# A two-layer graph-attention kernel on one core: layer 1's sums placed next to the head products, PSUM places given out anew, and the turn of h moved within the step

## The chip, the cores and the metric

The kernel runs on one core of one Trainium2 chip. The metric is the device time of the program in microseconds (us), as a median of several executions. One further execution was recorded by the hardware profiler; its own time and span stand beside the median below. The engines are named as in the profile: PE (matrix products and transposes; PEld is its loading of weights), DVE (vector engine), ACT (scalar engine), POOL (GpSimd) and SP (which issues DMAs).

## The reference

The input is x, 16 graphs of 1024 nodes with 256 features each, and adj, a 1024 x 1024 integer matrix of 0 and 1 for each graph. Two layers follow each other, each with a layer norm and a ReLU ahead of it and a residual around it.

Layer 0 is masked attention with 8 heads of 32 features:

```python
h = jnp.maximum(_layernorm(x), 0.0)
Q, K, V = proj(Wq, bq), proj(Wk, bk), proj(Wv, bv)      # 8 heads of 32
scores = einsum('bhnd,bhmd->bhnm', Q, K) * SCALE
scores = where(adj == 0, -inf, scores)
out = einsum('bhnm,bhmd->bhnd', softmax(scores), V)
x = x + out @ Wo.T + bo
```

Layer 1 has scores that are made of the nodes themselves, one kind of score for each value of adj (with adj of 0 and 1 only one kind occurs, and the kernel holds a slower way for the others that is not taken):

```python
h = jnp.maximum(_layernorm(x), 0.0)
e = leaky_relu(einsum('bid,bjd->bij', h * a_0[:, 0], h), 0.2)
x = x + softmax(where(adj == 1, e, -9e15)) @ h
```

## The kernel before

A *tile* is 128 rows (nodes) of one graph; there are 8 tiles in a graph and 128 in all. The kernel is one software pipeline over tiles, written out by hand (`tc.manual_schedule()`): the instructions of each engine are executed in just the order in which the program emits them. The outer loop runs over tile steps s (lines 839 to 980), the inner one over the 8 heads h of the tile that is now attended, which I call head steps. In each head step several objects at different stages do a piece of their work:

- `now` (class `Attend`) is the tile s whose heads are scored. `scores(h)` (L461) puts 128 x 1024 scores on one of two PSUM sides, `softmax_max(h)` (L473, DVE) takes them from there with the mask, and `softmax_exp` (L490, ACT) follows one head step later. Heads 4 and 6 use one side, the others the other side, so the scores of a head wait until L473 of the last head on the same side is done.
- Two head steps after its scores, a head's probabilities are turned. Heads 0, 1, 4 and 5 are turned by DVE in blocks (L381) and put in place by DMAs on SP (L386); heads 2, 3, 6 and 7 by PE (L590) with copies on ACT (L591). In the last tile of a graph (tile 7) PE turns heads 4 and 5 too, and in tile 0 heads 0 and 1; their exps then change the order of elements.
- `combine(0)` (L526) makes the products of heads 0 to 3 with the values in head step 7; `was.combine(1)` makes those of heads 4 to 7 in head step 3 of the next tile step, after `recT` (L520), the reciprocals of the sums. Both use the array in 32 columns at a time (128*32 in the profile). `combined` (L536) multiplies, `output` (L541) makes y in head step 4, `residual` (L547) and `norms` follow on DVE in head step 5.
- `piece` (class `Piece`) is the tile 9 steps ahead, whose Q, K and V are made. `normed` (L223, ACT, head step 4) makes h, `turn` (L237, PE, head step 5) transposes it, `turned` (L249 and L250, ACT) copies it out twice as hT and hTm, `project(0, ...)` (L267, head step 6) makes K, `raised(0)` (L309, ACT, head step 7) takes K out of PSUM. As `piece_was` it goes on in the next tile step: Q by `project(1, ...)` in head step 1, taken out by `raised(1)` (L309) in head step 4, and V by `values` (L344) in head step 2, taken out by `biased` (L355).
- `edge` and `edge_was` (class `Edges`) are layer 1's tiles 9 and 10 steps behind. `edge` has its scores made (L627 and L633), its maximum taken (L656), bent (L665), its copies kept for the mirrored half (L647) and its exp (L680). `edge_was` has its probabilities turned in head step 0, and its sums are made by `gather(0)` and `gather(1)` (L698, 64 matmul instructions together in the profile, also 32 columns at a time). `store` (L705, L707 on DVE, L708 on SP) divides, adds the residual and sends the result out.

The mask of the next tile is made by `flag` (L453, ACT) and `mask` (L441, POOL) in head step 3. Gathers exist from s = 10 on; the piece ends with s = 118. After the loop a tail does layer 1 for the last graph's tiles.

PSUM is given out by hand: the two score sides, two rotating buffers for transposes, and two banks of two places each for all that is smaller. A wait between engines holds for a whole bank:

```python
banks = [ps_acc.tile([P, 2, D], F32, tag=f"acc{i}", ...) for i in range(2)]
sums_place, brief, early, late = (banks[i // 2][:, i % 2, :] for i in range(4))
```

Before the change, `sums_place` takes the head products and the gathers' sums, `brief` the turned h of layer 1 and the turned reciprocals, `early` Q, and `late` V, y, the turned h of the piece, and K.

Of the kernel before, what the change touches and what calls it, by code (L numbers as in the profile page):

```python
# [17 lines left out]
P = 128  # L18
# [12 lines left out]
def by_blocks(t):  # L31
    return BY_BLOCKS.get(t, MIXED)
# [15 lines left out]
def gnn_kernel(  # L48
# [46 lines left out]
    sums_place, brief, early, late = (banks[i // 2][:, i % 2, :] for i in range(4))  # L95
# [92 lines left out]
    class Piece:  # L188
# [66 lines left out]
        def project(self, which, oc):  # L255
            wT, bias = ((weights["wkT"], bk_t), (weights["wqT"], bq_t))[which]
            b, w = self.b, self.n * P
            if b not in kds:
                kds[b] = dram.tile([NC, P, 2, N], F32, tag="kd", name=f"kd_{b}")
            if b not in qds and which == 1:  # L260
                qds[b] = dram.tile([NT, NC, P, 2, 2, P], F32, tag="qd", name=f"qd_{b}")
            if self.n > 1:
                ps = ps_tr.tile([P, w], F32, tag="tr", name="proj")
            else:
                ps = (late, early)[which][:, oc * P : (oc + 1) * P]
            for fc in range(NC):
                nc.tensor.matmul(  # L267
                    ps,
                    lhsT=wT[:, fc, oc * P : (oc + 1) * P],
                    rhs=(self.hT, self.hTm)[which][:, fc, :],  # L270
                    start=(fc == 0),
                    stop=(fc == NC - 1),
                )

            self.projected.append((which, oc, ps, bias))
# [139 lines left out]
    class Attend:  # L415
# [120 lines left out]
            nc.vector.tensor_tensor(self.oT, by_chunk(sums_place), self.recT, ALU.mult)  # L536

        def output(self):
            self.y = late
            for g in range(NC):  # L540
                nc.tensor.matmul(  # L541
                    self.y, lhsT=self.oT[:, g, :], rhs=weights["woT"][:, g, :], start=(g == 0), stop=(g == NC - 1)
                )
# [50 lines left out]
    class Edges:  # L594


        def __init__(self, b, t, last=False):
            self.b, self.t, self.last = b, t, last
            self.rows = slice(t * P, (t + 1) * P)
            self.side = sides[t % 2 if last else 1]  # L600
            self.tags = {"sel": ("p", 4), "pT1": ("pT", 7)} if last else {}
            if last and t % 2:
                self.tags |= {"ha": ("hT", 1), "x1b": ("x1", 1), "h0": ("xb", 1)}
            self.sums = late if last and t % 2 else sums_place

        def buffer(self, tag, shape):
            tag, bufs = self.tags.get(tag, (tag, 1))
# [168 lines left out]
    def attend_of(s):  # L776
        return Attend(*divmod(s, NT)) if 0 <= s < B * NT else None
# [9 lines left out]
    with tc.manual_schedule():  # L787
        first = [Piece(0, 0, 4), Piece(0, 4, 4)]
        piece_was, piece_next = Piece(1, 0), piece_of(0)
        now, nxt = attend_of(0), attend_of(1)  # L790
# [39 lines left out]
        piece, edge, edge_was = piece_next, None, None  # L830
# [8 lines left out]
        for s in range(B * NT + 1):  # L839
            b, t = divmod(s, NT)  # L840

            def load_keys(h, end):
                if t == NT - 1 and b + 1 < B and 2 * h + end in KEY_STEPS:
                    load_key(b + 1, KEY_STEPS.index(2 * h + end))
                if t == 0 and 0 < b < B and 2 * (HEADS + h) + end in KEY_STEPS:
                    load_key(b, KEY_STEPS.index(2 * (HEADS + h) + end))

            nxt2, edge_nxt, piece_nxt = attend_of(s + 2), edges_of(s + 1), piece_of(s + 1)
            for h in range(HEADS):
                ending, eh = (now, h - 1) if h >= 1 else (was, HEADS - 1)  # L850
                turning, th = (now, h - 2) if h >= 2 else (was, HEADS + h - 2)

                load_keys(h, 0)


                if now:
                    now.scores(h)
                if h == 0 and piece_was:
                    piece_was.halve(0)
                if s == 0 and h == 1:  # L860
                    first[1].values()
                if h == 3 and edge:
                    edge.softmax_max()
                if h == 5:
                    if was:
                        was.residual()
                    norms(was, piece_nxt)
                if h == 6 and edge_was:
                    edge_was.gather(1)
                if now:  # L870
                    now.softmax_max(h)
                if h == 6 and edge_was:
                    edge_was.store()


                if h == 1 and edge:
                    edge.keep(0)
                if h == 2 and gone:
                    gone.turned_normed()
                if ending:  # L880
                    ending.softmax_exp(eh)

                if h == 3 and was:
                    was.turned_reciprocals()
                if h == 3 and edge:
                    edge.bend()
                    edge.keep(1)


                if h == 3:  # L890
                    if was:
                        was.combine(1)
                    if piece_was:
                        piece_was.biased()
                    if was:
                        was.combined()
                if turning and th in by_blocks(turning.t):
                    turning.turn_blocks(th)
                    turning.place_blocks(th)
                elif turning:  # L900
                    turning.turn(th, 0)
                    turning.turn(th, 1)


                if h == 0:
                    if edge:
                        edge.score(0)
                    if gone:
                        gone.normed()
                    if edge_was:  # L910
                        edge_was.turn_blocks()
                        edge_was.place_blocks()
                if h == 1:
                    if gone:
                        gone.turn_normed()
                    if piece_was:
                        piece_was.project(1, 0)
                        piece_was.project(1, 1)
                    if was:
                        was.reciprocals()  # L920
                    if piece_nxt:
                        piece_nxt.load()
                if h == 2:
                    if edge:
                        edge.score(1)
                    if piece_was:
                        piece_was.values()
                    if was:
                        was.turn_reciprocals()
                        was.add_bias()  # L930
                if h == 3:
                    if nxt:
                        nxt.load_queries()
                    if edge:
                        edge.leak()
                    if edge_was:
                        edge_was.load_nodes()
                    if nxt:
                        nxt.flag()
                        nxt.mask()  # L940
                if h == 4:
                    if was:
                        was.output()
                    if piece_was:
                        piece_was.raised(1)
                        piece_was.halve(1)
                    if piece:
                        piece.normed()
                    if piece_was:
                        piece_was.write_queries()  # L950
                    if edge_nxt:
                        edge_nxt.prepare()
                    if nxt2:
                        nxt2.load()
                if h == 5:
                    if edge_was:
                        edge_was.gather(0)
                    if piece:
                        piece.turn()
                    if piece:  # L960
                        piece.turned()
                if h == 6:
                    if edge:
                        edge.softmax_exp()
                    if was:
                        was.keep()
                    if now:
                        now.load_nodes()
                    if piece:
                        piece.project(0, 0)  # L970
                        piece.project(0, 1)
                if h == 7:
                    if now:
                        now.combine(0)
                    if piece:
                        piece.raised(0)
                load_keys(h, 1)
            gone, was, now, nxt = was, now, nxt, nxt2
            edge_was, edge = edge, edge_nxt
            piece_was, piece = piece, piece_nxt  # L980
# [84 lines left out]
```

## Time and profile before

| | |
|---|---|
| median of 3 runs | 3068.4 us (3067.28 to 3073.23) |
| the profiled execution | 3076.4 us |
| its span in the trace | 3074.5 us, 96254 instructions |
| mean granted clock of TensorE | 0.996 |
| L461, scores, x2048 | 760.6 us busy |
| L590, transposes of probabilities, x4608 | 604.5 us busy |
| L526, head products, x16384 | 533.4 us busy |
| L698, gathers, x8192 | 496.9 us busy |
| L473, maximum on DVE, x1024 | 1236.2 us busy |
| L490, exp on ACT, x1024 | 1249.4 us busy |

The table is read as follows. The span is the time from the first to the last instruction of the profiled execution. Busy time is the time in which at least one instruction of the group ran. PE's matmuls overlap, and their ends are modelled, so the distance between two starts says more of PE than a duration does. In the answers of the trace a line gives a start in us from the begin of the span, a duration, the engine, the line of the program, the operation, what it writes and reads, and how many instructions are merged in it. "[0.67 <-PE s L461]" says that the engine had been idle for 0.67 us and which result ended that.

### The profile page before, as it was taken

The page shows a single profiled execution, that of the slowest core. Times are in us where ns is not written, and L with a number is a line of the kernel's source. Part 1 is how long each engine was busy: PE and PEld are TensorE (multiplying, and loading weights), DVE is VectorE, ACT ScalarE, POOL GpSimd, SP SyncE. Part 2 cuts the span into 40 slices and gives each one's busy share as a digit, 9 for nine tenths or more (in the row PEclk, how much of TensorE's full clock was granted, in tenths as well). Part 3 has the DMA queues.
Part 4 walks back from the last instruction along what each step waited for, and adds up shares of the span by engine and source line. Part 5 has one row for each costly group of instructions (what it writes and reads, how often), then busy time and mean ns, then how long its engine had stood idle before and what let it go on. Part 6 is the DMA issues. An engine that isn't in the chain of part 4 may idle for free. (4 is left out here: it accounts for less than half of the span.)

```text
span 3074.5 us, 96254 instructions
## 1 busy us (share of the span) xinstructions
PE 2965.6 (96%) x36722; PEld 2230.1 (73%) x36722; DVE 2515.6 (82%) x4453; ACT 2654.5 (86%) x5159; POOL 2177.6 (71%) x2999
## 2 busy tenths in 40 slices
PE   7889999999999999999999999999999999999998
PEld 5667777777777777777777777777777777776664
DVE  5878888888888888888888788888888888888885
ACT  5888888899898998889889888988989888898882
POOL 3657777777777777777777777777777777776542
PEclk9999999999999999999999999999999999999999
DMA  7766777877777786777777777787777777777653
GB/s 245 219 219 205 237 235 222 255 216 243 231 225 243 230 257 209 232 247 220 246 230 228 235 232 243 221 255 221 220 247 228 251 211 235 237 227 236 191 168 100
DMA packets 597828, 695.68 MB, mean 226 GB/s; under 512 B 63280, under 2 KB 528560, under 8 KB 597360
## 3 DMA queue, kind: packets, MB, share of 16 engines
q1 hardware_dynamic: 528288, 477.29, 51.9%
q0 software_dynamic: 66960, 210.04, 21.0%
q8 instruction: 295, 4.83, 0.7%
q10 hardware_dynamic: 2112, 2.10, 0.2%
q14 instruction: 173, 1.42, 0.1%
HBM read 252.98 MB, written 134.22 MB: 126 GB/s over the span
## 5 line engine op out<-in xcount | busy, mean ns | idle before, releaser
L473 DVE CUSTOM_DVE_ANT_0 p<-s,neg 128x1024 f32<-128x1024 f32 x1024 | 1236.2, 1208 | 220.7 <-PE s L461 185.1
L490 ACT ACTIVATE p<-p,nmx 128x1024 f32<-128x1024 f32 x1024 | 1249.4, 1224 | 132.5 <-DVE nmx L473 123.9
L461 PE MATMUL s<-k,qt 128*128 128x512 f32 x2048 | 760.6, 453 | 15.5 <-DVE nmx L473 4.3
L591 ACT COPY pT<-trp 128x512 f32<-128x512 f32 x1024 | 549.4, 590 | 95.3 <-PE trp L590 94.9
L590 PE MATMUL trp<-ident,p 128*128 128x128 f32 x4608 | 604.5, 274 | 4.7 <-ACT pT L591 1.5
L590 PEld LDWEIGHTS trp<-ident,p 128*128 128x128 f32 x4608 | 531.0, 140 | 104.0 <-ACT pT L591 10.8
L381 DVE STREAM_TRANSPOSE blocks<-p 128x1024 f32<-128x1024 f32 x456 | 564.5, 1238 | 12.3 <-ACT p L680 10.6
L526 PE MATMUL acc<-pT,v 128*32 128x128 f32 x16384 | 533.4, 275 | 41.8 <-ACT recT L520 30.0
L526 PEld LDWEIGHTS acc<-pT,v 128*32 128x32 f32 x16384 | 453.5, 110 | 153.0 <-ACT recT L520 85.0
L698 PE MATMUL acc<-h,pT 128*32 128x256 f32 x8192 | 496.9, 382 | 2.8 <-DVE h L707 1.7
L441 POOL TENSOR_SCALAR neg<-adj 128x1024 bf16<-128x1024 int32 x128 | 467.9, 3655 | 42.9 <-ACT neg L453 33.7
L461 PEld LDWEIGHTS s<-k,qt 128*128 128x128 f32 x2048 | 322.9, 191 | 106.3 <-issue 43.0
L698 PEld LDWEIGHTS acc<-h,pT 128*32 128x32 f32 x8192 | 241.8, 109 | 207.8 <-issue 65.6
L676 POOL TENSOR_TENSOR sel<-sel,less 128x1024 f32<-128x1024 f32 x120 | 286.8, 2390 | 68.9 <-ACT less L665 47.6
L633 PE MATMUL s<-h1T,ha 128*128 128x512 f32 (+2 forms) x744 | 272.8, 490 | 2.7 <-ACT h1T L569 1.6
L674 POOL TENSOR_SCALAR less<-top 128x1 f32<-128x1 f32 x120 | 31.9, 266 | 274.0 <-DVE top L656 273.9
L324 POOL DMA_DIRECT2D qd<-halves x240 | 177.5, 780 | 58.7 <-POOL halves L314 31.8
L490 ACT ACTIVATION_READ_ACCUMULATOR p<-p,nmx 128x1 f32 x1024 | 206.8, 202 | 0.0
L510 POOL COPY wide<-rec 128x256 f32<-128x256 f32 x128 | 53.8, 420 | 204.2 <-DVE rec L508 204.2
L330 POOL DMA_DIRECT2D kd<-halves x240 | 172.2, 766 | 35.5 <-POOL halves L314 35.4
L314 POOL TENSOR_TENSOR halves<-full,halves 128x256 fp32r<-128x256 f32 x240 | 176.8, 737 | 20.6
L633 PEld LDWEIGHTS s<-h1T,ha 128*128 128x128 f32 x744 | 126.7, 190 | 70.7 <-issue 45.0
(117 smaller groups left out, 4328.4 us busy)
## 6 DMA issues: line engine op xcount, KB each, us to landing
pT<-blocks SPq DMA_DIRECT2D x2304, 128.0 KB, 3.5
qt<-qd SPq DMA_DIRECT2D x128, 512.0 KB, 4.5
k<-kd SPq DMA_DIRECT2D x128, 512.0 KB, 7.3
adj<-in_adj POOLq DMA_DIRECT2D x127, 512.0 KB, 5.0
qd<-halves POOLq DMA_DIRECT2D x240, 256.0 KB, 2.7
kd<-halves POOLq DMA_DIRECT2D x240, 128.0 KB, 4.1
xb<-in_x POOLq DMA_DIRECT2D x128, 128.0 KB, 4.2
x1d<-x SPq DMA_DIRECT2D x128, 128.0 KB, 4.0
```

Source lines behind the costliest of these rows:

```text
L324: nc.gpsimd.dma_start(out=qds[self.b][self.first, oc].rearrange("p u w n -> p u (w n)"), in_=halves.unsqueeze(1).to_broadcast([P, 2, 2 * P]),)
L381: nc.vector.transpose(blocks.rearrange("p b j q -> p j b q"), p)
L441: nc.gpsimd.tensor_scalar(self.neg, self.adj, 0.0, MASKED, ALU.is_equal, ALU.mult)
L461: nc.tensor.matmul(self.ps[:, cols], lhsT=self.qt[:, h, :], rhs=keysets[self.b][h][:, cols], start=True, stop=True,)
L473: nc.vector.tensor_tensor_reduce(out=p, in0=sides[h in self.second], in1=self.neg, scale=-SCALE, scalar=FLOOR, op0=ALU.add, op1=ALU.min, a ...
L490: nc.scalar.activation(to, of, AF.Exp, bias=nmx, scale=-1.0, accum_out=self.sums[:, h : h + 1])
L526: nc.tensor.matmul(sums_place[r * HD : (r + 1) * HD, g * P : (g + 1) * P], lhsT=vs[self.b][:, j, place_of(h) : place_of(h) + HD], rhs=self ...
L590: nc.tensor.transpose(tr[:, j, :], p[:, jj * P : (jj + 1) * P], ident)
L591: copy(pT[:, half * 4 : half * 4 + 4, :], tr)
L633: nc.tensor.matmul(self.side[:, cols], lhsT=self.ha[:, c, :], rhs=h1T[:, c, cols], start=(c == 0), stop=(c == NC - 1),)
L676: nc.gpsimd.tensor_tensor(self.sel, self.sel, self.less, ALU.subtract)
L698: nc.tensor.matmul(self.sums[a * HD : (a + 1) * HD, :], lhsT=self.pT[:, j, a], rhs=h1s[self.b][:, j, :], start=(j == 0), stop=(j == NT - 1),)
```

## The change

The change is in the order of emission and in the PSUM places; what is computed stays the same, and no instruction is added or dropped.

- Both gathers and the store move to head step 7. Before, `gather(0)` stood in head step 5 behind head 3's transposes, `gather(1)` in head step 6 behind the scores, and the store in head step 6. Now they stand together, directly ahead of `combine(0)`; K is made in head step 7 too, ahead of the gathers, and taken out (`raised(0)`) after the store.
- The places: the gathers' sums go to `early` (in the second bank), y and the piece's K to `brief` (in the first).
- `turn` and `turned` of the next h move ahead of head 3's transposes in head step 5, so L237 directly follows the scores of head 5 on PE, and L249 and L250 go ahead of head 3's copies on ACT.
- `softmax_max` moves ahead of residual and norms in head step 5.

On PE the order from head step 5 on was scores 5, L590, L698, L237, scores 6, L698, L267, scores 7, L526. It is now scores 5, L237, L590, scores 6, scores 7, L267, L698, L698, L526. In tile 7 the transposes of heads 4 and 5 stand directly behind scores 6 and 7.

```diff
@@ project
-                ps = (late, early)[which][:, oc * P : (oc + 1) * P]
+                ps = (brief, early)[which][:, oc * P : (oc + 1) * P]
@@ output
-            self.y = late
+            self.y = brief
@@ Edges
-            self.sums = late if last and t % 2 else sums_place
+            self.sums = (late if t % 2 else sums_place) if last else early
@@ the loop over heads
+                if now:
+                    now.softmax_max(h)
                 if h == 5:
                     if was:
                         was.residual()
                     norms(was, piece_nxt)
-                if h == 6 and edge_was:
-                    edge_was.gather(1)
-                if now:
-                    now.softmax_max(h)
-                if h == 6 and edge_was:
-                    edge_was.store()
...
+                if h == 5 and piece:
+                    piece.turn()
+                    piece.turned()
                 if turning and th in by_blocks(turning.t):
...
-                if h == 5:
-                    if edge_was:
-                        edge_was.gather(0)
-                    if piece:
-                        piece.turn()
-                    if piece:
-                        piece.turned()
                 if h == 6:
...
                     if now:
                         now.load_nodes()
+                if h == 7:
                     if piece:
                         piece.project(0, 0)
                         piece.project(0, 1)
-                if h == 7:
+                    if edge_was:
+                        edge_was.gather(0)
+                        edge_was.gather(1)
+                        edge_was.store()
+                    if piece:
+                        piece.raised(0)
                     if now:
                         now.combine(0)
-                    if piece:
-                        piece.raised(0)
```

## The prediction

> **What bounds the kernel now.** I read the busy shares first, then PE's order of time in one tile step (one pass of the loop over s), then the same step on ACT and DVE, then the waits.
>
> ```profile
> PE 2965.6 (96%) x36722; PEld 2230.1 (73%) x36722; DVE 2515.6 (82%) x4453; ACT 2654.5 (86%) x5159; POOL 2177.6 (71%) x2999
> ```
>
> PE has the least air, and in the timeline one of its groups follows the other. The step from 1455.26 us, head steps 5 to 7 and then the next step's head 0 (columns: start, duration, engine, line):
>
> ```profile
> 1455.26 0.81 PE L461 MATMUL s<-k,qt 128*128 128x512 f32 x2
> 1455.91 1.03 PE L590 MATMUL trp<-ident,p 128*128 128x128 f32 x8
> 1456.88 1.93 PE L698 MATMUL acc<-h,pT 128*32 128x256 f32 x32
> 1458.74 0.44 PE L237 MATMUL acc<-ident,h 128*128 128x128 f32 x2
> 1458.94 0.71 PE L461 MATMUL s<-k,qt 128*128 128x512 f32 x2
> 1459.58 1.93 PE L698 MATMUL acc<-h,pT 128*32 128x256 f32 x32
> 1461.44 1.16 PE L267 MATMUL acc<-hT,wkT 128*128 128x128 f32 x8
> 1462.36 0.71 PE L461 MATMUL s<-k,qt 128*128 128x512 f32 x2
> 1463.00 1.95 PE L526 MATMUL acc<-pT,v 128*32 128x128 f32 x64
> 1464.89 0.73 PE L461 MATMUL s<-k,qt 128*128 128x512 f32 x2
> ```
>
> From start to start (that is what PE pays) no group waits here. The narrow groups (128*32) come three times, each between wide ones (128*128). Ordinary steps (tiles 2 to 6 of a batch) repeat every 22.1 to 22.7 us, so a microsecond on this path is a microsecond of the step. On ACT, in the same step:
>
> ```profile
> 1455.90 0.65 ACT L309 ACTIVATE full<-acc,bq_t 128x128 f32<-128x128 f32 x2
> 1456.41 0.62 ACT L223 ACTIVATE h<-xin,shift,r 128x256 f32<-128x256 f32 x1
> 1456.90 1.16 ACT L490 ACTIVATE p<-p,nmx 128x1024 f32<-128x1024 f32 x1
> ```
>
> L223 makes the h that L237 turns. It ends at 1457.03, and L237 ran at 1458.74: 1.7 us of cover, given by head 3's transposes (L590) and the first gather (L698). The change takes both away.
>
> **Saved on PE: passages between narrow and wide.** Starts to starts, L590 takes 0.97 ahead of L698, but 0.87 ahead of a wide group (1465.46 to 1466.33); a score pair takes 0.64 ahead of a narrow group, 0.55 ahead of a wide one (1446.25 to 1447.07 and on to 1447.61 shows 0.82 for a projection and 0.54 for the pair). A gather of 32 takes 1.86. In the tail both gathers already run as one:
>
> ```profile
> 3019.12 3.66 PE L698 MATMUL acc<-h,pT 128*32 128x256 f32 x64 [1.74 <-DVE h L707]
> 3022.71 0.55 PE L627 MATMUL s<-ident,mirror 128*128 128x128 f32 x3
> ```
>
> 3.59 to the next wide group, against 2 x 1.86 = 3.72; followed by L526, narrow too, it also saves the passage out, 0.11 (within a gather four matmuls start every 0.216, the last four are followed by a wide start after 0.33): 3.48. New order from L237 to the next step's head 0: L237 0.22, L590 0.79 (0.08 less ahead of scores, as two transposes of L516 take 0.14 there), scores 6 0.63 (ahead of scores 7; no such neighbours in the trace, bounds 0.46 and 0.65, two starts 0.316 apart is what a pair shows inside), scores 7 0.55, L267 0.98, gathers 3.48, L526 1.87: 8.52. Before, L590 to head 0 is 1464.89 - 1455.91 = 8.98. **Saved 0.45 a step** (0.40 to 0.55). 109 tile steps (s = 10 to 118) have both gather and turn: **-49 us**.
>
> **Added: PE waits for h.** In the new order L237 follows scores 5, so it could start at 1455.91. L223 ends at 1457.03, and PE starts 0.05 after an ACT result (recT to L526, all 128 times): 1457.08. PE stands still for 1.17, and everything behind L237 with it: head 3's transposes, scores 6 and 7, gathers, products. Over all 120 turns the end of L223 lies 0.91 to 1.32 behind the start of the group after scores 5, mean 1.09. One part goes: L309 read `early` and waited for L541 writing `late` in the same bank; y is now in the other bank. Waits name it, "ACT full L309 <- PE acc L541", 8.5 us in all, 0.06 a step. **1.09 - 0.06 + 0.05 = 1.08; x 109 = +118 us.** Does ACT come earlier when PE is slower? The chain into L223 starts at PE's own scores 2:
>
> ```profile
> 1470.26 1.23 DVE L473 CUSTOM_DVE_ANT_0 p<-s,neg 128x1024 f32<-128x1024 f32 x1 [0.67 <-PE s L461]
> ```
>
> ```profile
> 1473.81 1.06 ACT L665 ACTIVATE less<-sel 128x1024 f32<-128x1024 f32 x1 [0.67 <-DVE top L656]
> ```
>
> From there L473, head 0's turn and L656 on DVE, then L665, mirror, mask flag, exp 3, two copies, L309, L223 on ACT run without a gap (in tile 0 with one of 1.0 for PE): 9.4 to 9.9 us from scores 2 to h. PE is waited for at its head, so the chain moves with PE and the wait repeats in each step.
>
> **Added: the batch's last tile.** In tile 7 heads 4 and 5 are turned by PE, and their exps, which change the order, take twice as long:
>
> ```profile
> 1501.70 2.26 ACT L490 ACTIVATE p<-p,nmx 128x1024 f32<-128x1024 f32 x1
> ...
> 1505.28 2.26 ACT L490 ACTIVATE p<-p,nmx 128x1024 f32<-128x1024 f32 x1
> ```
>
> ```profile
> 1506.43 1.09 PE L590 MATMUL trp<-ident,p 128*128 128x128 f32 x8
> ...
> 1508.72 1.03 PE L590 MATMUL trp<-ident,p 128*128 128x128 f32 x8
> ```
>
> Both L590 now find exp ready, because the gathers go ahead of them. Laid out anew: L309 has 0.29 less wait, so h at 1501.51, L237 1501.56, head 3 1501.78, scores 6 1502.57, turn of head 4 at 1503.17; exp 4 runs from 1501.41 to 1503.67, so 1503.72: 0.55 lost. Scores 7, then the turn of head 5 at 1505.06; exp 5 starts after exp 4 (2.11), L249, L250 (0.53) and two copies (0.94) at 1504.99 and ends 1507.25: 1507.30, 2.24 lost. **2.8 x 13 tiles = +36 us.**
>
> **Without gathers (s = 0 to 9).** Today L267 waits 1.64 there for hTm, which now comes ahead of head 3's copies; but L526 directly follows L267 and must wait for L309: both are in the first bank. From 118.05: h 119.33, L237 119.38, L267 to 122.35, exps 5 and 6 and L309 to 124.75, L526 124.80, next head 0 at 126.69 against 127.31: **-6 us** in all. Where gathers stand between them, L309 ends 0.13 before the gathers (1463.61 and 1463.74 by the rows above): no wait. The last nine steps have no turn: -4, and two tiles 7 with exp waits, +5: **+1**.
>
> The rows behind that bank wait are L309's 27 waits for L541, which write and read different columns. The Trainium skill, PSUM — Partial Sum Buffer, section "PSUM bank collisions raise a hardware error", says why: PSUM is to be guarded by bank and quadrant, not by address. That speaks against K in `brief` beside the products in `sums_place`; by address alone the first ten steps would be 2.25 faster each.
>
> **The rest at nothing.** L473 of head 5 goes ahead of residual and norms (1.55 on DVE): it ends near 1457.3, scores 7 need its side at about 1458.4; behind the 1.55 it would cost 0.4. L707 and L705 now stand right ahead of head 0's L473 on DVE: gathers end near 1463.8, L707 done by 1464.6, the scores that L473 needs land near 1466.3. On SP the store (L708) moves behind L552 and eight L386 loads and ahead of the sel blocks' four, whose data come over 2 us later; POOL gets head step 7's L309 earlier against head 0 (1.9 instead of 1.1).
>
> **Clock.** Long gaps lower it: with the 1.64 wait at 122 us the mean is 0.92, later 1.00.
>
> ```profile
> 119.00:140.00 21.00, 17.80 (x210) 14.62 (x209) 16.60 (x29) 17.39 (x37) 13.08 (x18) 0.92 0.67 208
> ```
>
> 8% of 21 us is 1.7 us. The same steps from 98 us show 1.00, so not every such wait does it. Tile 7's 2.24 may: 0 to 25 us for 15; I take **+10**, under a half.
>
> The Trainium skill, TensorE: Matmul & The Clock Gate, section "Why this matters for your kernels", asks only that gaps stay under about 3 us; by it this term is 0 and the sum 100. The row above contradicts that, so I keep the 10.
>
> **Sum:** -49 + 118 + 36 - 6 + 1 + 10 = **+110 us** on the profiled 3076.4, 3186; the runs' median 3068.4 is 8.0 lower: **3178 us**.
>
> **Rivals.**
> - *More waits* (0.14): L309 comes 0.4 later than laid out (margin 0.13); L526 waits 0.3 x 109 = 33 and the clock takes 25: 3226. For it: ACT is the fullest engine after PE. Against: DVE leaves it nothing to wait for in this stretch.
> - *h earlier* (0.14): ACT gains until only L541 holds L223 (1500.59 + 0.10 + 0.60 + 0.05 against 1500.90: 0.44 wait); 0.64 x 109 = 70 less: 3108. Against: ACT shows no gap between L665 and L309 in most steps.
> - *Faster* (0.08): h is there when scores 5 end. It decides once L237's wait is under 0.45, the saving. With no waits at all: 3068.4 - 49 - 6 = 3013. Against: 0.91 is the least seen.
> - *It doesn't do what it says* (0.04): waits inside the narrow run cancel the 0.45 and h hides: 3068.
>
> **Numbers.** Forecast 3178 with 0.60. Range 3095 to 3235: it takes in the unknowns (scores 6, clock, L309: 3140 to 3230) and the first two rivals, 0.88. Under 0.2%, 6 us, a measurement can't tell from no change: faster 0.08, same 0.04, slower 0.88.
>
> **What would show it.** Ordinary steps near 23.1 instead of 22.4; L237 and its weights idle some 1.1 us "<-ACT h L223"; L590 idle in tiles 7 behind ACT p; L698 x64 then L526 in one run of about 5.3. Wrong if L237 starts within 0.3 of scores 5, or if L526 waits for L309 in ordinary steps.

## The result, and the profile after

The changed kernel takes 3184.72 us (median of 4 runs, 3179.14 to 3185.3), the one before 3070.16 us in the runs beside it: a ratio of 1.0369, 95% interval 1.0351 to 1.0387. The prediction, 3178 us, lies 7 us below. The profiled execution has a span of 3183.5 us against 3074.5, at the same mean granted clock of 0.996.

The busy shares of the changed kernel, from its page:

```profile
PE 2938.4 (92%) x36722; PEld 2276.2 (71%) x36722; DVE 2511.9 (79%) x4453; ACT 2625.8 (82%) x5159; POOL 2177.5 (68%) x2999
```

Every engine has a smaller share of the span than before, and only PEld is busy for longer (2276.2 us against 2230.1), so the time went into waits. The timeline of PE in an ordinary step of the changed kernel, the same stretch as the one shown of before (start, duration, engine, line; in brackets the idle time ahead of the group and what ended it):

```profile
1515.08 0.82 PE L461 MATMUL s<-k,qt 128*128 128x512 f32 x2
1516.90 0.44 PE L237 MATMUL acc<-ident,h 128*128 128x128 f32 x2 [1.00 <-ACT h L223]
1517.17 1.04 PE L590 MATMUL trp<-ident,p 128*128 128x128 f32 x8
1517.97 1.18 PE L461 MATMUL s<-k,qt 128*128 128x512 f32 x4
1518.98 1.05 PE L267 MATMUL acc<-hT,wkT 128*128 128x128 f32 x8
1519.97 3.66 PE L698 MATMUL acc<-h,pT 128*32 128x256 f32 x64
1523.45 2.16 PE L526 MATMUL acc<-pT,v 128*32 128x128 f32 x64
1525.54 0.73 PE L461 MATMUL s<-k,qt 128*128 128x512 f32 x2
```

The first row starts at 1515.08, the second at 1516.90: 1.82 us for a group that takes 0.65. L237 waits for L223's h, as forecast. The gathers and the head products now run as one stretch of narrow matmuls, and from L698 to L526 it is the 3.48 of the forecast. L526 takes 2.09 to the next scores, though, where 1.87 was laid out. Why is seen in the waits (who waited, for what; us in total, times, longest):

```profile
PEld acc L237 <- ACT h L223: 162.1, 119, 1.9
...
PEld acc L526 <- ACT full L309: 53.6, 106, 3.6
```

```profile
PE acc L237 <- ACT h L223: 110.4, 119, 1.4
```

```profile
1522.74 0.66 ACT L309 ACTIVATE full<-acc,bk_t 128x128 f32<-128x128 f32 x2
```

The first line is the forecast wait, in 119 of the 120 turns. The second was forecast for the first ten steps alone: L526's weights wait for L309, K's taking out, in 106 steps. In the step above L309 ends at 1523.40 by its line, and L526 starts at 1523.45, 3.48 after the gathers. That is no wait to speak of, but the run of L526 takes 0.2 longer to the next scores.

In tile 7 PE waits twice more, in the two places that the forecast names:

```profile
1566.19 1.14 PE L590 MATMUL trp<-ident,p 128*128 128x128 f32 x8 [1.25 <-ACT pT L591]
...
1568.72 1.09 PE L590 MATMUL trp<-ident,p 128*128 128x128 f32 x8 [0.91 <-ACT p L490]
```

The second of these waits is for head 5's slow exp. The first is for head 3's copy, which stands behind head 4's slow exp on ACT and holds the buffer that the transposes of head 4 need.

The steps, from one tile's scores 5 to the next tile's, medians of 13 or 14 graphs:

| tile | 0 | 1 | 2 | 3 | 4 | 5 | 6 | 7 |
|---|---|---|---|---|---|---|---|---|
| before | 23.78 | 23.05 | 22.73 | 22.45 | 22.47 | 22.17 | 22.28 | 26.09 |
| changed | 23.76 | 23.55 | 23.66 | 23.40 | 23.40 | 22.98 | 23.14 | 29.56 |

### The profile page after: what moved, and what is told of

Its sections match the earlier page's. It is cut to its first block, busy times and chain, and to the rows that moved or that the text cites. A ratio compares the mean times of both kernels' runs of the same rounds, so it can differ in the third digit from the quotient of the medians.

```text
span 3183.5 us, 95926 instructions
## 1 busy us (share of the span) xinstructions
PE 2938.4 (92%) x36722; PEld 2276.2 (71%) x36722; DVE 2511.9 (79%) x4453; ACT 2625.8 (82%) x5159; POOL 2177.5 (68%) x2999
## 5 line engine op out<-in xcount | busy, mean ns | idle before, releaser
L591 ACT COPY pT<-trp 128x512 f32<-128x512 f32 x1024 | 553.4, 597 | 337.8 <-PE trp L590 337.6
L461 PE MATMUL s<-k,qt 128*128 128x512 f32 x2048 | 732.8, 447 | 14.6 <-DVE nmx L473 5.1
L590 PE MATMUL trp<-ident,p 128*128 128x128 f32 x4608 | 606.5, 274 | 37.4 <-ACT pT L591 20.9
L590 PEld LDWEIGHTS trp<-ident,p 128*128 128x128 f32 x4608 | 526.6, 140 | 126.2 <-ACT pT L591 37.1
L526 PE MATMUL acc<-pT,v 128*32 128x128 f32 x16384 | 547.6, 276 | 53.5 <-ACT recT L520 30.3
L526 PEld LDWEIGHTS acc<-pT,v 128*32 128x32 f32 x16384 | 470.8, 110 | 153.5 <-ACT recT L520 85.2
L698 PE MATMUL acc<-h,pT 128*32 128x256 f32 x8192 | 473.1, 381 | 1.6 <-DMA pT<-blocks 1.5
L461 PEld LDWEIGHTS s<-k,qt 128*128 128x128 f32 x2048 | 329.9, 190 | 110.0 <-issue 41.5
L698 PEld LDWEIGHTS acc<-h,pT 128*32 128x32 f32 x8192 | 255.3, 110 | 179.2 <-DMA pT<-blocks 6.8
L490 ACT ACTIVATION_READ_ACCUMULATOR p<-p,nmx 128x1 f32 x1024 | 221.3, 216 | 0.0
```

The costliest lines, as they stand in the source:

```text
L461: nc.tensor.matmul(self.ps[:, cols], lhsT=self.qt[:, h, :], rhs=keysets[self.b][h][:, cols], start=True, stop=True,)
L490: nc.scalar.activation(to, of, AF.Exp, bias=nmx, scale=-1.0, accum_out=self.sums[:, h : h + 1])
L526: nc.tensor.matmul(sums_place[r * HD : (r + 1) * HD, g * P : (g + 1) * P], lhsT=vs[self.b][:, j, place_of(h) : place_of(h) + HD], rhs=self ...
L590: nc.tensor.transpose(tr[:, j, :], p[:, jj * P : (jj + 1) * P], ident)
L591: copy(pT[:, half * 4 : half * 4 + 4, :], tr)
L698: nc.tensor.matmul(self.sums[a * HD : (a + 1) * HD, :], lhsT=self.pT[:, j, a], rhs=h1s[self.b][:, j, :], start=(j == 0), stop=(j == NT - 1),)
```

## The experiments

My theory at first was the forecast's: L237's wait for h costs the step its length. The rivals were that L237 waits for something else too, and, after the first experiment, that the step is set by another chain. The ratios are against the kernel before, which ran beside each of them (medians 3072 to 3080 us).

**1. The price of a passage, in the kernel before.** One passage from narrow to wide matmuls and back is added, by cutting the first gather in two.

```diff
-                        edge_was.gather(0)
+                        edge_was.gather(0, 0)
                     if piece:
                         piece.turn()
+                    if edge_was:
+                        edge_was.gather(0, 1)
```

> The kernel before with the turn of h (L237) between the two halves of the first gather instead of behind it: the same instructions, one narrow run more in each of 109 steps. Theory (each passage into and out of a narrow run costs PE 0.2 to 0.35 us): +22 to +38 us, 3100 us. Rival (a passage costs nothing by itself): 3066 to 3076.

Measured: 3100.11 us, ratio 1.0092 (1.0075 to 1.0109): +28 us in 109 steps, 0.26 a step; single steps grow by 0.31 in the median. The saving that the forecast counts on is real.

**2. The turn of h behind head 3's transposes again.** Everything else stays as changed, and ACT's order too.

```diff
-                    piece.turn()
-                    piece.turned()
+                    between = piece
...
+                        turning.turn_around(th, between)
...
+            for half in range(2):
...
+            piece.turn()
+            piece.turned()
+            for half, tr in enumerate(trs):
+                copy(pT[:, half * 4 : half * 4 + 4, :], tr)
```

> The changed kernel with one thing undone: on PE the turn of h (L237) stands behind head 3's eight transposes again; on ACT its two copies stay ahead of head 3's. Theory (PE stands still for h): 0.87 us of transposes cover the wait, which falls from 1.08 to some 0.2 in 96 ordinary steps, -83 us; nothing in tiles 7, where the turn of head 4 waits for its exp at the same time as before; -6 in the first ten steps: 3096 us (3080 to 3115). Rival (the 6.5 us from scores 7 to the next scores 0, in which PE makes no scores, starve DVE and ACT): that stretch is unchanged, so 3175 to 3190.

Measured: 3199.43 us, ratio 1.0413 (1.0392 to 1.0434), 15 slower than the changed kernel. Here my first theory fell. PE in an ordinary step (a new function stands in this program, and the lines behind it are higher by 15: L506, in it, is head 3's transposing, L511 its copies, L713 are the gathers, L541 the head products, L605 the other transposes):

```profile
1545.50 0.82 PE L461 MATMUL s<-k,qt 128*128 128x512 f32 x2
1546.16 1.03 PE L506 MATMUL trp<-ident,p 128*128 128x128 f32 x8
1547.53 0.44 PE L237 MATMUL acc<-ident,h 128*128 128x128 f32 x2 [0.34 <-ACT h L223]
...
1550.01 3.66 PE L713 MATMUL acc<-h,pT 128*32 128x256 f32 x64
1554.09 2.16 PE L541 MATMUL acc<-pT,v 128*32 128x128 f32 x64 [0.41 <-ACT full L309]
```

L237's wait fell as meant: scores 5 to scores 6 takes 2.12 instead of 2.99. But the gathers, which take 3.48 to what follows, are now followed after 4.08, and scores 7 to the next scores 0 takes 7.90 instead of 7.02. An ordinary step takes 23.40 as it did. What L237 no longer waits, the head products wait for K.

Of the 15 us, 12 are tile 7's: its 13 steps lose 57 us against before, where the changed kernel loses 45. There PE now waits in one long piece, and the granted clock falls behind it:

```profile
1573.61 1.22 PE L605 MATMUL trp<-ident,p 128*128 128x128 f32 x8 [2.09 <-ACT pT L511]
...
1576.15 1.95 PE L605 MATMUL trp<-ident,p 128*128 128x128 f32 x8 [0.47 <-ACT p L490]
```

The eight transposes of the second line take 1.95 us, where the changed kernel takes 1.09. The clock is 0.51 from 1574.5 to 1577.9 us. Such a stretch of half clock stands in 12 of the 13 tiles 7. It is 3.4 us long, in three of them 6.8, and just these three are 2 us longer than the others. The one tile 7 without it takes 29.56, as in the changed kernel. The mean clock is 0.986 or 0.987 in all four runs, and 0.995 to 0.998 in those of the changed kernel.

The two waits hang on one chain. PE's scores 2 release DVE's work, that releases ACT, and ACT then works without a gap through L223 (h), exp 4, the copies, exp 5, L680, exp 6, to L309 (K). The table gives, for tile 3, the time from scores 2 to the end of L223, from scores 2 to the end of L309 for K (of the second of its two instructions), from there to the next step's scores 2, and the step:

| kernel | scores 2 to h | scores 2 to K | K to next scores 2 | step |
|---|---|---|---|---|
| before | 10.08 | 16.72 | 5.73 | 22.45 |
| changed | 10.07 | 16.62 | 6.78 | 23.40 |
| 2, turn behind head 3 | 10.07 | 16.63 | 6.78 | 23.40 |
| 3, h early | | 16.18 | 6.78 | 22.96 |
| 4, h and Q early | | 16.16 | 6.78 | 22.94 |
| 5, K ahead of exp 6 | 10.07 | 15.49 | 7.67 | 23.17 |
| 8, 2 and 5 together | 10.07 | 15.50 | 7.08 | 22.58 |
| 7, all three | | 15.03 | 7.18 | 22.22 |

The revised theory: the ordinary step is the longest of three rounds. One is PE's own work. One goes from scores 2 over h and L237 back to scores 2. One goes from scores 2 over K and L526 back to scores 2; where it binds, the last part is 6.78, what PE takes from L526's release to scores 2. In the changed kernel the last two are nearly equal, and that is why taking one away gains little.

**3. h alone made earlier.** L223 moves to head step 3, with a buffer of its own for h; the pool `small` has three buffers instead of four here and in 4, 7 and 10.

```diff
+                if h == 3 and piece:
+                    piece.normed()
                 if h == 3 and edge:
                     edge.bend()
...
-                    if piece:
-                        piece.normed()
```

> As the kernel with both moved, but only h (L223) is made in head step 3; Q is taken out (L309) in head step 4 as before. If a wait goes by PSUM bank, L237, which writes late, still waits for L309, which reads early in the same bank and ends some 0.5 us before L223 did: 0.58 of 1.08 remain, -50 to -55 us: 3131 us (3115 to 3145). If it goes by address, L237 waits no longer: 3067 us, as with both moved. Starved DVE and ACT: 3165 to 3185.

Measured: 3142.94 us, ratio 1.0227 (1.0205 to 1.0249). L237's weights now wait for "ACT full L309", Q's taking out, 113.1 us in 119 waits: the wait by bank, since the turned h goes to the other half of Q's bank. It is 12 above the first figure: scores 5 to scores 6 fell from 2.99 to 2.54 only, and from K on the step takes 6.78, so K's round binds here.

**4. h and Q both earlier.**

```diff
+                if h == 3 and piece_was:
+                    piece_was.raised(1)
+                if h == 3 and piece:
+                    piece.normed()
                 if h == 3 and edge:
                     edge.bend()
...
-                        piece_was.raised(1)
...
-                    if piece:
-                        piece.normed()
```

> The changed kernel with Q's way out (L309) and h (L223) made in head step 3 ahead of L665, where ACT waits for L656; h gets a buffer of its own. Theory (PE stands still for h): L237 never waits; 96 x 1.08 = -104 in ordinary steps, 13 x 0.6 = -8 in tiles 7 (the rest of their loss is the wait for exps), -6 at the start: 3067 us (3050 to 3085). Rival (starved DVE and ACT): 3165 to 3185, since the order on PE is the same.

Measured: 3134.33 us, ratio 1.0205 (1.0184 to 1.0226), a miss by 67 us. L237 waits no more at all: scores 5 to scores 6 takes 1.66. But:

```profile
PEld acc L526 <- ACT full L309: 94.9, 93, 4.1
...
PEld s L461 <- ACT mirror L647: 44.4, 99, 0.6
```

K's round binds (16.16 + 6.78), and scores 3 to scores 4 takes 3.14 instead of 2.79: the mirror copy L647, which frees the score side, now stands behind L309 and L223 on ACT.

**5. K taken out ahead of head 6's exp.**

```diff
-                if ending:
+                if ending and not (h == 7 and now and piece):
                     ending.softmax_exp(eh)
...
                         piece.raised(0)
+                        if now:
+                            now.softmax_exp(6)
```

> The changed kernel with K's way out (L309 in head step 7) ahead of the exp of head 6 on ACT, some 1.1 us earlier. In the changed kernel the head products (L526) take 2.09 us to the next scores instead of 1.89, and the wait of their first weights is put down to L309. Theory (that wait, just over when L526 comes, still costs 0.2, as the wait for recT does in L526 of head step 3): 1.89 again in 104 steps, -21, and 10 x 1.1 = -11 where no gathers stand between: 3153 us (3145 to 3162). Rival (the 0.2 comes of the long narrow run or of K beside the sums in one bank): only the first ten steps gain, 3172 to 3178.

Measured: 3151.35 us, ratio 1.0254 (1.0237 to 1.0271), as expected. L526 waits for L309 in only ten steps, and its run is back at 1.86, 1523.35 to 1525.21:

```profile
1523.35 1.93 PE L526 MATMUL acc<-pT,v 128*32 128x128 f32 x64
1525.21 0.73 PE L461 MATMUL s<-k,qt 128*128 128x512 f32 x2
```

The nine steps after the first fall from 202.3 to 191.1 us, the ordinary step by 0.23 to 23.17. That is h's round alone, so K's round was 0.23 the longer one.

**6. Tile 7: heads 4 and 5 turned behind the gathers.**

```diff
-                elif turning:
+                elif turning and not (th in (4, 5) and edge_was):
...
                         edge_was.gather(1)
+                        if now and 4 not in by_blocks(now.t):
+                            for late_h in (4, 5):
+                                now.turn(late_h, 0)
+                                now.turn(late_h, 1)
```

> The changed kernel, but in the last tile of a graph the transposes of heads 4 and 5 stand behind the gathers, ahead of the products of heads 0 to 3. Theory (PE waits for two slow exps there): 2.8 us less in 15 such tiles, one more passage between narrow and wide of 0.35: -37 us, 3148 us (3138 to 3158). Rival (those waits only stand in for a lack that the next tile would show anyway): 3175 to 3190.

Measured: 3162.68 us, ratio 1.0295 (1.0275 to 1.0315). Tile 7's step falls from 29.56 to 28.19 and no other step changes: 1.4 x 13 is 18 of the 22 us. It was to be more. Behind the gathers the transposes of head 5 wait 0.44 for DVE's copies (L591), in all 13 tiles 7, and the two runs of transposes together take 2.62 (1560.94 to 1563.56) where 1.74 would do without a wait. K is not the cause: L309 ends some 1.25 before L526 starts.

**7. All three (4, 5 and 6 together).**

```diff
+                    piece_was.raised(1)
+                    piece.normed()
...
+                            now.softmax_exp(6)
...
+                                now.turn(late_h, 0)
```

> Three moves together on the changed kernel: Q out and h in head step 3, tile 7's heads 4 and 5 behind the gathers, K out ahead of the exp of head 6. If the waits are all that the change cost, what is left is the saving on passages: 3185 - 118 - 37 - 32 = 2998, and from the kernel before, 3070 - 49 - 6 = 3015: 3005 us (2985 to 3035), faster than both kernels. If PE's stretch without scores costs by itself (head 0's maximum late, ACT's copies late), more than 3060.

Measured: 3050.10 us, ratio 0.9933 (0.9916 to 0.9949): faster than both kernels, but 45 above what was expected. PE in an ordinary step:

```profile
1511.44 0.82 PE L461 MATMUL s<-k,qt 128*128 128x512 f32 x2
1512.10 0.38 PE L237 MATMUL acc<-ident,hp 128*128 128x128 f32 x2
...
1513.10 1.21 PE L461 MATMUL s<-k,qt 128*128 128x512 f32 x4
1514.15 1.05 PE L267 MATMUL acc<-hT,wkT 128*128 128x128 f32 x8
...
1520.47 0.73 PE L461 MATMUL s<-k,qt 128*128 128x512 f32 x2
```

Scores 6 and 7 are one row here. This is the new order without a wait. From scores 5 to the next scores 0 it takes 9.03; before took 9.63 (1464.89 - 1455.26). So the change is worth 0.60 a step on PE, not 0.45. Most of the 45 us are the 0.35 of the mirror copy in tiles 0 to 3 (less in the others), and tile 7, still 1.3 above before in each of 13 steps.

**8. Edits 2 and 5 together.** This tells the revised theory from one in which the two waits are separate costs.

```diff
+                        turning.turn_around(th, between)
...
+                            now.softmax_exp(6)
```

> The changed kernel with both edits that did little alone: L237 behind head 3's transposes on PE (alone +15 us) and L309 of K ahead of head 6's exp on ACT (alone -33 us). Theory (the wait of L237 for h and the wait of L526 for L309 stand one behind the other on the same chain of ACT, so each fills in for the other): scores 5 to scores 6 stays at 2.12 as with the first edit alone, scores 7 to the next scores 0 falls from its 7.90 to the 6.79 of the second, an ordinary step takes 22.30 instead of 23.40; with tile 7 at 30.05 and the first ten steps at 193 together 3075 us. Rival (two separate costs that add): 3185 + 15 - 33 = 3166 us, ordinary steps 23.2.

Measured: 3102.1 us, ratio 1.0094 (1.0071 to 1.0118). Alone the edits gave +15 and -33 us; together they give -83, and the ordinary step falls by 0.82. So they are not separate costs. The size was missed by 27 us, and the waits say by what:

```profile
PEld acc L267 <- ACT hT L249: 40.6, 92, 1.2
PEld acc L237 <- ACT h L223: 38.6, 82, 0.6
```

L267, now right behind scores 7, waits for hT, and scores 7 to scores 0 takes 7.07 instead of 6.79. Some 7 us more stand in three of the tiles 7, which take 31.66 to 32.25 instead of 29.5: the wait of 2.08 is there as in experiment 2, and in these three half clock follows for 6.8 us.

**9. The turn ahead of head 3's transposes, alone, in the kernel before.** There L526 has no K to wait for.

```diff
+                if h == 5 and piece:
+                    piece.turn()
+                    piece.turned()
                 if turning and th in by_blocks(turning.t):
...
                         edge_was.gather(0)
-                    if piece:
-                        piece.turn()
-                    if piece:
-                        piece.turned()
```

> The kernel before with one part of the change alone: L237 (and L249, L250 on ACT) ahead of head 3's transposes in head step 5; gathers, places and K's taking out stay where they were. There L526 has no L309 ahead of it on ACT, so nothing stands in for L237's wait. Theory (the wait for h costs its full length where no second wait on the same ACT chain is there to absorb it): L237 waits 1.08 us in each of 109 to 118 steps, +118 to +127, less some 5 in the first ten steps, where hT comes earlier: 3187 us, scores 5 to scores 6 at 4.7 instead of 3.68. Rival (the step is set by a loop over ACT of about 23.4 us that the wait only fills, as taking the wait away with the changed kernel gave nothing): ordinary steps stay within 0.3 of 22.4, 3072 to 3105 us.

Measured: 3202.78 us, ratio 1.0401 (1.0384 to 1.0418), +123 us, steps of tiles 2 to 6 longer by 1.3 to 1.45. Where nothing stands in for it, the wait costs its whole length, and more than I priced. The profile says what is added:

```profile
1512.47 0.82 PE L461 MATMUL s<-k,qt 128*128 128x512 f32 x2
1514.41 0.41 PE L237 MATMUL acc<-ident,h 128*128 128x128 f32 x2 [1.12 <-DVE x L547]
```

L223 ended at 1514.23. L237 went 0.13 later than that would have allowed, because here it writes `late`, from which L547 reads y. L547 starts 0.09 after L309 has read Q from the same bank (median of 109 steps), 1.12 after y is made, so it is L309 that it had waited for. So about 0.13 of the 1.44 isn't h's. Together with 2: moving the turn costs 1.3 a step where h's round is the only one, and going back gains nothing where K's round is as long.

**10. Version 7 with L223 ahead of head 2's exp and Q's L309 behind the mirror copy.**

```diff
+                if h == 3 and piece:
+                    piece.normed()
                 if ending and not (h == 7 and now and piece):
                     ending.softmax_exp(eh)
...
                     edge.keep(1)
+                if h == 3 and piece_was:
+                    piece_was.raised(1)
```

> The version with all three edits, with L223 moved on to stand ahead of head 2's exp (ACT idles 0.67 behind that exp, for recT) and L309 of Q behind the mirror copy L647, so that the mirror copy comes 1.0 earlier. Theory (scores 4 wait for the mirror copy there, 3.14 us from scores 3 to scores 4 against 2.79): this falls to 2.79 in tiles 0 to 3 and by 0.1 to 0.25 in 4 and 5, 24 us in all, 3026 us. Rival (ACT's order only moves the wait: recT comes 0.5 later behind L223, and L526 of heads 4 to 7 with it): 3050 us, no change against the version with all three.

Measured: 3057.76 us, ratio 0.9949 (0.9932 to 0.9966), 8 above version 7. Scores 3 to scores 4 is back at 2.80, as the theory has it. The waits name what ate the gain:

```profile
DVE v L355 <- ACT full L309: 87.1, 105, 1.0
```

V's taking out on DVE now waits for Q's on ACT; both read the same bank. Tile 7 loses 0.9 and the nine steps after the first 13 us, with the clock down to 0.93 between 100 and 150 us, where version 7 has 1.00, and with two waits for loads of qt, 3.76 and 2.09 us, where version 7 has 1.30 at most. Tiles 0 and 1 gain 0.35. So the rival came nearer, though recT wasn't the place.

## Why the prediction was right

The sum was +110 and the spans differ by 109.0. Much of this agreement is owed to errors that cancel.

- **Passages, -49:** right in kind, and mis-sized. By version 7 it is 0.60 a step, -65. It lies above the 0.40 to 0.55 that I gave: the two score pairs take 1.05 up to L267 (1513.10 to 1514.15), where 1.18 was laid out.
- **L237 waits for h, +118:** shown by its 119 waits and by experiment 9. Scores 5 to scores 6 takes 1.66 without the wait; in the changed kernel it is above that by 0.6 in tile 0, 0.9 in tile 1, 1.2 to 1.4 in the others, 1.19 in the mean: +129. That ACT's chain moves with PE and the wait repeats was right: scores 2 to h is 10.07 or 10.08 (tile 3) in every kernel that leaves it in place.
- **Tile 7, +36:** measured 2.45 x 13 = +32. The split was off. I had 0.55 for head 4 and 2.24 for head 5; it is 1.35 and 1.10, since head 4's transposes wait for their PSUM buffer behind head 3's copies, not for the exp.
- **L526 waits for K, 0 in ordinary steps:** this is the step that failed, and the text named it as what would make it wrong. I laid L309's end 0.13 ahead of the gathers' end; it is 0.05 ahead of L526's start, and the run of L526 takes 0.2 more in tiles 1 to 6, +16 us. More than its size, its place was missed: K hangs on the same chain as h, which made the forecast's main term one that can't be had back by itself.
- **Sum of the main part:** -65 + 129 + 32 + 16 = +112, measured +102.4 (steps 10 to 118). An ordinary step takes 23.40, where the sign given was 23.1; tile 0's did not grow at all, since its wait is no longer than the saving. Eight of the ten left are in six single steps, in which the difference is 0.8 to 1.8 below that of the same tile elsewhere. In those six the kernel before has a wait of its own, in the run of L526 for heads 4 to 7 ("<-DMA pT<-blocks", 0.67 to 1.61 us), which the changed kernel does not have.
- **First ten steps, -6:** measured +10.5. Of these 2.9 lie ahead of the first scores 5, before any turn of the loop, where PE's longest wait is for a load of k (3.32 against 1.42 before). 1.4 come in the first step, where L237 waits 1.42 and L526 2.28, and 6.1 in the nine others. Experiment 5 shows what the wait for K, which I had priced, costs there: without it the nine take 191.1 us instead of 202.3. The saving of 6 isn't shown: before took 196.2, but the same instructions took 191.1 in experiment 1, which does not touch these steps.
- **Last steps, +1:** measured -3.8.
- **Clock, +10:** measured 0. From 300 us on the granted clock is 1.00 in both kernels. The term was for one wait of 2.24 in tile 7, which came as two, of 1.35 and 1.10. In experiment 2 it is one wait of 2.09, and there the clock does fall.
- **Rivals:** "h earlier", "faster" and "it doesn't do what it says" didn't occur. "More waits" named the right wait, with 33 us where it has 16, and a clock loss that did not come.

In the changed kernel, one early step shows L526 behind L267 without gathers between them:

```profile
126.14 1.05 PE L267 MATMUL acc<-hT,wkT 128*128 128x128 f32 x8
129.48 2.16 PE L526 MATMUL acc<-pT,v 128*32 128x128 f32 x64 [2.29 <-ACT full L309]
```

L526 writes the first half of the bank, L309 reads the second. The forecast drew this wait from the Trainium skill, PSUM — Partial Sum Buffer, section "PSUM bank collisions raise a hardware error". The same section also asks that two engines that only read one bank be kept apart; experiments 9 and 10 show what that costs here, 0.13 us a step on PE and 0.98 on DVE ("ACT full L309" in the step at 1571 us).

## What to carry to other kernels

When a wait on the path goes, ask which round, from a release back to the same release, is the next longest; two waits on results of one in-order engine stand in for each other, and removing one alone may show nothing. Cut such waits together, or move the makers on the engine that both hang on: here taking K out ahead of one exp and making h a head step earlier turned 3.7% slower into 0.7% faster. Small margins between two engines' ends (here 0.05 us) are no margin: the run behind them takes longer all the same (2.09 us against 1.86).

## What the hardware showed that I had not expected

- The same 64 narrow matmuls of L526 take 1.86 to the next group when their last operand has long been ready (experiment 5) and 2.09 when it is released at the last moment, with an idle time of next to nothing ahead of them. The run for heads 4 to 7, whose weights wait for recT in all 128 steps, shows the same (1510.88 to 1512.96 in the changed kernel, 2.08). I did not settle why.
- Waits of 0.9 to 1.4 us on PE, one in each step, and two more in tile 7, left the granted clock at 1.00 over 2700 us, and so did waits of 1.6 to 1.8 in the tiles 7 of experiment 4. Waits of 2.08 to 2.11 did not: half clock set in around the end of such a wait in 12 of 13 tiles 7 of experiment 2, and in 3 of 13 of experiment 8. Between 190 and 270 us, before the steps are full, the mean clock was 0.92 in the changed kernel, behind waits of 2.29, 2.33 and 3.41, and 0.96 before, behind waits of 1.64. The Trainium skill, TensorE: Matmul & The Clock Gate, section "Why this matters for your kernels", asks that idle gaps of PE stay under about 3 us. By these rows that limit is too wide here: waits of 1.64 and of 2.1 were followed by half clock, though not every time. What decides it was not tested.
